# A graph-network layer on one core: three loads and one sum change their engine or their place

## The chip, the core and the metric

The kernel runs on one core of a Trainium2 chip. A time is the device time of one execution in microseconds (us). The kernel before took 1768.54 us, the median of three runs (1767.38 to 1768.69).

The engines are named as in the profile: PE is TensorE (matmuls; PEld its weight loads), DVE is VectorE, ACT is ScalarE, POOL is GpSimd, SP is SyncE. SP computes nothing here: it issues DMAs. ACT and POOL issue some as well, between their other instructions.

## The reference, cut to what matters

The input is 32 graphs of 512 nodes with 256 features, and a 0/1 adjacency matrix for each. All is float32.

```python
h = max(layernorm(x), 0)
# convolution branch: 1x1, then 17 taps along the nodes
c = relu(bn1(conv1(h)));  c = bn2(conv2(c));  x_conv = relu(c + h)
# message branch
s = h @ w_se.T + b_se                       # 3 features
A = exp(-|s_n - s_m|^2) * adj
x_nmp = A @ relu(h @ w_msg.T + b_msg)
# GRU over both
gi = concat(x_conv, x_nmp) @ w_ih.T + b_ih
gh = h @ w_hh.T + b_hh
r = sigmoid(gi_r + gh_r);  z = sigmoid(gi_z + gh_z)
n = tanh(gi_n + r * gh_n)
out = x + (1 - z) * n + z * h
```

## The kernel before, in words

The 32 graphs are worked on in two groups of 16 (`GB = 16`), and the 17-tap convolution is done in the frequency domain. The order of the instructions on each engine is the order of the Python program: inside `tc.manual_schedule()` nothing is moved. So each engine, and each DMA queue, is a list that is worked through from the front, and an instruction that waits holds back what stands behind it.

The stages, in order of time:

- **First part of group 0** (`first_part(0, ...)`, from the start to about 158 us). For each graph `b`: x is loaded (`load_x`), layer-normalised (`statistics` on DVE with one power on POOL, L370; `normalise` on DVE, L383), transposed on PE (`transpose_h`, L391), cut at zero into `hT` on DVE (L395), multiplied by conv1's weights (`conv1`, L411; the bias is added on DVE, L414) and transformed by windows (`windows_to_freq`, L426). The graphs are staggered: the statistics of graph `b + 2` are computed while graph `b` is in `conv1`. Between these, conv2's weights are transformed: 32 steps of `weights_to_freq` (eight matmuls each, L335), which the function `between(b)` deals out over the graphs. Their input comes in eight pieces (`load_taps`, L322 and L323), in two buffers of the tag `w2p`. Conv1's weights (`w1_in`, loaded by `load_w1`, L188) pass through one of these buffers too, before `scale_w1` (L269) folds the batch norm into `w1`.
- **Nodes of group 0** (about 158 to 434 us): the message branch, with the frequency-domain products of the units 0 to 35 between its steps.
- **First part of group 1** (about 432 to 550 us), with the same functions. The last four units of group 0, `u0` to `u3`, are left over, and their products (`product`, L475) are the list `left`, dealt out by `fill()`: they keep PE busy while the pipeline of group 1 fills. A product needs its weights `wt` (`load_unit`, L437, issued by SP), the sum of their two halves (`sum_unit`, POOL, L442) and the sum of two factors (POOL, L455). In the same stage the GRU's weights are loaded and combined for a fast matrix product (`combine_weights`, a list of 15 entries, called from L1225). Its entry 0 is only the load of `w_hh` (four DMAs on SP, L188); the entries behind it are sums on POOL, copies on ACT and stores.
- **Nodes of group 1** (about 550 to 831 us).
- **Gates** (from about 831 us to the end): for each of 16 pairs of graphs, 26 products (`gates_rz26`, L868), whose operands are blocks of the inputs or sums of blocks. `block_sum` computes these sums on POOL (L771 and L773). For the first pair they are ordered by `FIRST_ORDER`: nine of the part `hn`, then `inverse(0)` (L833 on PE, L837 on DVE, L839 on ACT), then the rest, which begins with `('t4', 'c')`. That is the index that the local name `ahead` holds.

SP's list around the left-over products follows from `first_part`, with `g = 1`: the load of the next x; `fill()` (the load of `u2`); another x; the store of `hT` (L396); `fill()` (the product of `u0`); `fill()` (the product of `u1` and the load of `u3`). The products store their results through ACT's queue.

## Time and profile before

| | us |
|---|---|
| median of three runs | 1768.54 |
| the profiled execution, its own time | 1767.84 |
| span of its trace, first to last instruction | 1766.1 |
| PE busy | 1749.3 (99%) |
| PE not busy | 16.8 |
| DVE, POOL, ACT busy | 1334.8, 1114.9, 674.9 |

The durations below come from the profiled execution; 1.7 us of its time lie outside the span. PE's granted clock was 0.999. Where PE is not busy can be read from a table of stages:

| stage, us | length | PE busy | DVE busy | POOL busy |
|---|---|---|---|---|
| 0 to 15 | 15 | 10.35 | 8.62 | 5.62 |
| 15 to 30 | 15 | 13.11 | 11.84 | 3.60 |
| 30 to 150 | 120 | 120.00 | 97.14 | 44.24 |
| 440 to 455 | 15 | 15.00 | 12.30 | 8.48 |
| 455 to 475 | 20 | 19.02 | 16.20 | 9.98 |
| 475 to 550 | 75 | 75.00 | 61.37 | 44.37 |
| 820 to 850 | 30 | 29.68 | 9.65 | 18.96 |
| 850 to 1700 | 850 | 850.00 | 636.62 | 532.12 |

### The profile page before, as it was taken

How to read it: one execution, taken by the hardware profiler on the slowest of the kernel's cores; microseconds unless marked ns; L12 is line 12 of the kernel's file. 1: busy time of each engine (PE TensorE's matmuls, PEld its weight loads, DVE VectorE, ACT ScalarE, POOL GpSimd, SP SyncE). 2: the span in 40 equal slices, each digit the busy share in tenths (PEclk: the TensorE clock that was granted, in tenths of full speed). 3: DMA queues.
4: the chain of work that ended last, by engine and by line, in shares of the span. 5: the costliest groups of instructions: out<-in, count | busy, mean ns of one | idle time of the engine just before them, and what ended most of it. 6: DMA issues, size and time to landing. Idle time of an engine off the chain costs nothing.

```text
span 1766.1 us, 24528 instructions
## 1 busy us (share of the span) xinstructions
PE 1749.3 (99%) x8054; PEld 1354.0 (77%) x8054; DVE 1334.8 (76%) x2621; ACT 674.9 (38%) x1543; POOL 1114.9 (63%) x1090
## 2 busy tenths in 40 slices
PE   8999999999999999999999999999999999999998
PEld 6777888888898888886877787778877787778754
DVE  7885877887896778776487778777877788777867
ACT  4556554543446445444323232223223232323221
POOL 3441787888555787777767556755766556755551
PEclk9999999999999999999999999999999999999999
DMA  9999997985779888888523453335423552345333
GB/s 250 317 297 224 246 245 225 240 224 183 260 249 221 249 237 241 225 236 278 171 71 64 116 126 93 79 80 125 121 64 67 125 126 73 70 108 125 103 59 71
DMA packets 311314, 295.16 MB, mean 167 GB/s; under 512 B 146940, under 2 KB 240668, under 8 KB 310804
## 3 DMA queue, kind: packets, MB, share of 16 engines
q1 hardware_dynamic: 301012, 265.77, 57.1%
q0 software_dynamic: 6736, 25.86, 4.6%
q10 hardware_dynamic: 3440, 1.97, 0.4%
q8 instruction: 64, 1.05, 0.3%
q14 instruction: 62, 0.51, 0.1%
HBM read 194.39 MB, written 99.16 MB: 166 GB/s over the span
## 4 chain that ended last, share of the span: by engine, by line
PE 95%; DVE 1%; POOL 1%; DMA 1%; ACT 1%; issue 0%; SPq 0%; ACTq 0%; POOLq 0%; DVEq 0%
PE pg L868 28%; PE pn L885 16%; PE py L475 12%; PE pn L630 10%; PE pm L526 6%; PE pc L411 5%; PE pc L833 5%; PE px L426 4%; PE pd L568 2%; PE pw L335 2%; PE phT L391 1%; PE pg L885 1%; PE pz L885 1%; PE psr L550 1%; DMA w<-in_w_hhT_dram 0%; POOL te L773 0%
## 5 line engine op out<-in xcount | busy, mean ns | idle before, releaser
L442 POOL TENSOR_TENSOR wsum<-wt 128x512 f32<-128x512 f32 x78 | 111.0, 1423 | 101.1 <-DMA wt<-wd 57.6
L475 PE MATMUL py<-wt,xf 128*128 128x256 f32 x640 | 154.2, 384 | 0.0
L868 PE MATMUL pg<-te,sw 128*128 128x256 f32 x600 | 154.0, 379 | 0.0
L475 PEld LDWEIGHTS py<-wt,xf 128*128 128x128 f32 x640 | 117.1, 190 | 34.9 <-issue 19.0
L859 ACT ACTIVATE rz<-rz,brz 128x256 f32<-128x256 f32 x180 | 86.3, 504 | 147.5 <-DVE rz L874 147.5
L578 DVE TENSOR_TENSOR A<-A,at 128x512 f32<-128x512 f32 x124 | 134.0, 1119 | 1.6 <-ACT A L574 1.6
L868 PEld LDWEIGHTS pg<-te,sw 128*128 128x128 f32 x600 | 114.0, 190 | 15.5
L868 PE MATMUL pg<-tn,sw 128*128 128x256 f32 x480 | 123.2, 379 | 0.0
L868 PE MATMUL pg<-hn,sw 128*128 128x256 f32 x480 | 123.2, 379 | 0.0
L885 PE MATMUL pn<-tn,sw_n 128*128 128x512 f32 x256 | 120.3, 592 | 0.0
L411 PE MATMUL pc<-w,hT 128*128 128x256 f32 x512 | 117.5, 382 | 0.9 <-DVE hT L395 0.5
L526 PE MATMUL pm<-wmsg,hq 128*128 128x259 f32 x512 | 117.5, 381 | 0.0
L1030 ACT ACTIVATE pn<-nt,vech 128x512 f32<-128x512 f32 x45 | 31.1, 692 | 218.7 <-DVE nt L1027 139.4
L411 PEld LDWEIGHTS pc<-w,hT 128*128 128x128 f32 x512 | 94.7, 190 | 23.6 <-issue 7.2
L771 POOL TENSOR_TENSOR tn<-hn 128x512 f32<-128x512 f32 x64 | 87.1, 1381 | 35.6 <-PE pn L885 35.6
L526 PEld LDWEIGHTS pm<-wmsg,hq 128*128 128x128 f32 x512 | 96.5, 189 | 14.7
L868 PEld LDWEIGHTS pg<-hn,sw 128*128 128x128 f32 x480 | 91.1, 190 | 18.3 <-PE pn L885 3.3
L370 POOL TENSOR_TENSOR rstd<-rstd,minus_half 128x4 f32<-128x4 f32 x32 | 33.3, 1041 | 108.4 <-DVE rstd L369 103.0
L868 PEld LDWEIGHTS pg<-tn,sw 128*128 128x128 f32 x480 | 91.2, 190 | 12.4
L874 DVE TENSOR_TENSOR ct<-pg,ct 128x256 f32<-128x256 f32 x180 | 74.7, 415 | 32.9 <-PE pg L868 23.5
L885 PEld LDWEIGHTS pn<-tn,sw_n 128*128 128x128 f32 x256 | 48.6, 190 | 61.2 <-issue 50.9
L833 PEld LDWEIGHTS pc<-back,yt 128*128 128x128 f32 x640 | 92.7, 190 | 1.3 <-issue 0.5
(225 smaller groups left out, 4431.4 us busy)
## 6 DMA issues: line engine op xcount, KB each, us to landing
wt<-wd SPq DMA_DIRECT2D x80, 512.0 KB, 6.8
adj<-in_adj_dram SPq DMA_DIRECT2D x128, 256.0 KB, 6.9
wd<-wst SPq DMA_DIRECT2D x64, 320.0 KB, 5.6
yd<-y SPq DMA_DIRECT2D x76, 256.0 KB, 5.8
yt<-yd SPq DMA_DIRECT2D x30, 640.0 KB, 6.2
hd<-hT SPq DMA_DIRECT2D x32, 512.0 KB, 5.2
nd<-nmp SPq DMA_DIRECT2D x32, 512.0 KB, 3.0
xb<-in_x_dram SPq DMA_DIRECT2D x128, 128.0 KB, 5.8
```

The lines of the kernel that those rows point to most:

```text
L411: nc.tensor.matmul(p[:, j, :], HT[b][:, ic, c * P : (c + 1) * P], w1[:, ic, :], start=(ic == 0), stop=(ic == DC - 1))
L442: nc.gpsimd.tensor_tensor(t, WT[g, u][:, 0], WT[g, u][:, 1], op=ALU.add)
L475: nc.tensor.matmul(dst, v[:, ic, :], w[:, ic, :], start=(ic == 0), stop=(ic == DC - 1))
L526: nc.tensor.matmul(p[:, : D + NS], hq[:, ic, c * P : (c + 1) * P], wmsg[:, ic, :], start=(ic == 0), stop=(ic == DC - 1))
L578: nc.vector.tensor_mul(A[b][:, mc, :], EXP.pop((b, mc)), AT.pop((b, mc)))
L630: nc.tensor.matmul(bk, left[:, k, :], right[:, k, :], start=(first and k == 0), stop=(k == 1), skip_group_check=True)
L771: nc.gpsimd.tensor_tensor(dst[:, k], x[:, k], y[:, k], op=op)
L833: nc.tensor.matmul(bk[:, t0:t1], YT[p][:, j, c, oc * P : (oc + 1) * P], back[:, n : n + t1 - t0], start=(c == 0), stop=(c == len(spans) - ...
L859: nc.scalar.activation(at(dst), at(src), AF.Sigmoid, bias=brz[:, o : o + 1], scale=sign)
L868: nc.tensor.matmul(bk, SW["hk"][:, k, s, :], c if k == 2 else hn[:, k], start=(onto is None and k == 0), stop=(k == K3 - 1), skip_group_ch ...
L874: nc.vector.tensor_tensor(at(dst), at(x), at(y), op=op)
L885: nc.tensor.matmul(bk[:, t], weight(q, k, o), terms[k][q][:, t], start=(first and i == 0), stop=(i == len(ks) - 1), skip_group_check=True)
```

## The change

It has four edits.

1. `load_w1` issues its four DMAs on POOL's queue instead of SP's. On POOL they stand ahead of `batch_norm("bn1")`; on SP the load of x of graph 1 and the first `load_taps` move up by four places.
2. `between` of group 0 gives graph 0 two steps of `weights_to_freq` instead of three, and graph 11 three instead of two. Of graph 0's two, one now comes ahead of the transposes of graph 1 (it was two). All steps between move one place back in the sequence.
3. Entry 0 of `combine`, the load of `w_hh`, is taken out of the list and put at the front of `left[1]`, ahead of the product of `u0`. `between` of group 1 counts from graph 2, so that the other entries stay with their graphs.
4. In `block_sum`, the one sum `('t4', 'c')` of pair 0 goes to DVE.

```diff
     def load_w1():
         t = W2P["w1"] = pools["gen"].tile([P, PI, D], FP, tag="w2p", name="w1_in", bufs=2)
-        load_rows(t[:, :DC], w1T, nc.sync)
+        load_rows(t[:, :DC], w1T, nc.gpsimd)
...
-        nc.gpsimd.tensor_tensor(dst, x, y, op=op)
+        (nc.vector if (p, name, part) == (0, *FIRST_ORDER[ahead]) else nc.gpsimd).tensor_tensor(dst, x, y, op=op)
...
-                n = (3, 0, *(3 if b == 6 else 2 for b in range(2, GB)))[b]
+                n = (2, 0, *(3 if b in (6, 11) else 2 for b in range(2, GB)))[b]
                 mine = [[steps.pop(0)] for _ in range(n)]
                 if b % 2 == 0 and b // 2 + 1 < QI // PI:
                     mine[b > 0].insert(0, partial(load_taps, gen, b // 2 + 1))
-                return (mine[0] + mine[1], mine[2:]) if b == 0 else mine
+                return (mine[0], mine[1:]) if b == 0 else mine
...
-                    return combine[b - 1] if 0 < b <= len(combine) else [], two
+                    return combine[b - 2] if 1 < b <= len(combine) + 1 else [], two
...
                 left = [[partial(load_unit, 0, u2, pools["sums"]), partial(prepare, pw, 0, u1, xf)],
-                        [partial(product, pw, 0, u0, xf), partial(prepare, pw, 0, u2, xf)],
+                        [*combine.pop(0), partial(product, pw, 0, u0, xf), partial(prepare, pw, 0, u2, xf)],
                         [partial(product, pw, 0, u1, xf), partial(load_unit, 0, u3)],
```

## The prediction

> **What bounds the kernel now.** The page first: PE is busy for 1749.3 of 1766.1 us, so everything but PE's idle 16.8 us is PE's own work, and the change removes no matmul. Then PE's waits, to find those 16.8 us.

> ```profile
> PE 1749.3 (99%) x8054; PEld 1354.0 (77%) x8054; DVE 1334.8 (76%) x2621; ACT 674.9 (38%) x1543; POOL 1114.9 (63%) x1090
> ```

> ```profile
> PE row L1133 <- DVE fr L302: 1.9, 1, 1.9
> PE phT L391 <- DVE xn L383: 1.9, 3, 1.1
> PE phT L391 <- ACT wst L345: 1.2, 1, 1.2
> PE pw L335 <- DMA w2p<-in_w2T_dram: 1.2, 1, 1.2
> ...
> PE pg L868 <- POOL tnc L773: 0.3, 1, 0.3
> ```

> The columns are total, count and longest wait. About 12 of the 16.8 us lie before the first products or behind the last ones. What the change can reach is three places. The timeline of PE in the first 32 us shows one:

> ```profile
> 9.99 3.72 PE L411 MATMUL pc<-w,hT 128*128 128x256 f32 x16 [0.50 <-DVE hT L395]
> 14.87 2.56 PE L335 MATMUL pw<-w2p,taps 17*80 17x512 f32 x16 [1.16 <-DMA w2p<-in_w2T_dram]
> ...
> 19.01 3.80 PE L411 MATMUL pc<-w,hT 128*128 128x256 f32 x16 [0.39 <-ACT wst L345]
> ...
> 29.79 1.64 PE L391 MATMUL phT<-ident,xn 128*128 128x128 f32 x8 [1.17 <-ACT wst L345]
> ```

> Behind the first conv1 PE idles 1.16 + 0.39 + 0.29 + 1.17 = 3.0 us, and never again before 165 us. The timelines of 428 to 482 us and 843 to 870 us show the others:

> ```profile
> 436.65 0.37 SPq L437 DMA_DIRECT2D wt<-wd  x1
> ...
> 445.82 1.27 POOL L442 TENSOR_TENSOR wsum<-wt 128x512 f32<-128x512 f32 x1 [0.39 <-DMA wt<-wd]
> ...
> 446.61 1.89 PE L475 MATMUL py<-wt,xf 128*128 128x256 f32 x8
> ...
> 464.17 1.28 POOL L1225 TENSOR_TENSOR w<-w 128x128 f32<-128x128 f32 x3 [4.69 <-DMA w<-in_w_hhT_dram]
> ...
> 469.45 0.69 PE L391 MATMUL phT<-ident,xn 128*128 128x128 f32 x2 [0.59 <-DVE xn L383]
> ...
> 847.82 0.70 PE L868 MATMUL pg<-tnc,sw 128*128 128x256 f32 x2 [0.32 <-POOL tnc L773]
> ```

> POOL waits 4.69 us for `w_hh`; the power L370 stands behind its sums, DVE's normalise behind that, and PE loses 0.98 us (20 less the 19.02 busy from 455 to 475). At 847.8 PE loses 0.32 us to the sum t4/c. Note also the last left-over weights: issued at 436.65, landed only at 445.7, used at 446.61. That load has 0.9 us to spare.

> [...] conv1's four issues hold SP from 1.67 to 4.90. [...] POOL's taps issued at 13.63 moved no packet until 17.0, when SP's backlog had run out; later the two queues shared. [...] The trace has the DVE product L578 at about 0.65 us (two in 1.29) and, beside POOL, at 1.75.

> **The start: conv1's weights and the moved step.** Removed from SP: 3.2 us of issue. The x of graph 1 leaves at 1.67 instead of 4.94, the first taps at 2.2 to 4.8 instead of 5.4 to 8.1. Added on POOL: four issues at 0.58 (row L322, 2.33 us for four), from about 1.3 to 3.6. Queued behind them is `batch_norm("bn1")`, which began at 3.26 on its vectors' arrival: it slips by some 0.4 us (0.6 if the first issue takes 0.74, as at 13.63). ACT takes its result at 4.85, so the row sums come some 0.4 later than 6.67; `scale_w1` uses them at 8.59. Covered. The x of graph 1 now competes with the second half of graph 0's x on ACT's queue at 3 to 4 us; I charge 0.3 us (0 to 0.6) to the chain from x to conv1.

> If conv1's weights land in time, by hand: conv1(0) runs 10.3 to 14.0. Graph 1's x is there, so its statistics follow hT at 10.25 (before: 0.76 us later, at 10.70, for the DMA), the power ends at 13.25, normalise 13.3 to 14.7. On PE: one step (1.03 us, from 1.10 for eight) 14.0 to 15.05, without the wait of 1.16, as the taps land about 3 us earlier, also if conv1's weights take 1 us of their bandwidth; the transposes of graph 1 to 16.1. DVE adds conv1(0)'s bias (1.28) to 15.95 and makes hT(1) to 17.3: PE idles 1.25 us and starts conv1(1) at 17.35. The second step ends at 22.0. On DVE the statistics of graph 2 run 17.3 to 19.2, POOL's power to 20.3, normalise to 21.75; bias to 23.0, statistics of graph 3 to 24.9, hT(2) to 26.2, normalise(3) to 27.6. PE's transposes of graph 3 therefore end near 28.4 and conv1(2) begins at 28.3, against 31.26. PE has then done one step less, 1.03 us, which it does at graph 11, where it is 100% busy. Gain: 31.26 - 28.3 - 1.03 = **1.9 us**. Behind that DVE still leads PE: xn(4) stood ready 2.6 us ahead of its use at 38.12, and PE moves up on DVE by some 0.9.

> The moved steps make the taps of pieces 2 and 3 wait for the last step on the old buffer, now behind conv1(2) and conv1(4). Queued behind them on POOL are a load of x and the power. Their issue slips from 34.1 to about 36 and from 49.6 to 53.9; the second delays the power at 57.18 by 1.0 us, its normalise at 58.86 by 0.5. DVE idles 0.96 + 0.42 us per graph there, and PE takes that xn only at about 65. Cost nothing; if that cover failed, under 1 us.

> Will conv1's weights land in time? `scale_w1` is due at 8.9. The landing times of the first 30 us:

> ```profile
> w2p<-in_w2T_dram SPq DMA_DIRECT2D x4, 128.0 KB, 7.0
> w2p<-in_w2T_dram POOLq DMA_DIRECT2D x4, 128.0 KB, 8.5
> ...
> w_in<-in_w1T_dram SPq DMA_DIRECT2D x4, 64.0 KB, 2.9
> ```

> The last POOL issue is at about 3.0. POOL's first packet came 1.6 us after issue on a quiet queue (444.61), 3.6 and 4.9 us after it behind a full SP queue (13.63, 812.79). With 0.7 us for the data and 0.8 to 2.6 to completion that gives 6.1 to 11.2. Lateness is paid in full, since hT, conv1 and graph 1's statistics stand behind `scale_w1` on DVE. Bounds: 0 to 2.3 us; I take 0.4, as the load leaves before the queues are full. **Start: -1.5 us**, from -2.2 to +0.7.

> **The load of w_hh.** It goes onto SP between the hT store (435.97) and the last left-over load (436.65). Four issues take 2.28 us, but the bytes matter more. From 433.0 to 443.4 the DMA engines moved 3.43 MB at 330 GB/s without a break, in SP's order, and the last left-over load was last. 786 KB ahead of it take 2.0 us at the best rate there, about 400 GB/s, or 3.7 us at the 211 GB/s of 459 to 462 us, where `w_hh` itself was moving. The load then lands at 447.7 to 449.4. PE waits for it from 446.61: 1.1 to 2.8 us, and 0.3 more for POOL's two sums (1.27 + 0.73), which now begin at the landing. Middle: 2.3 us lost. Queued behind on POOL are a load of x and the power of graph 19, which have the same delay as PE. Given back: POOL's 4.69 and PE's 0.98 us. **Sum: +1.3 us**, from +0.4 to +2.1; if the transfers don't delay that load at all, -1.0.

> **The first gate sum.** POOL takes 1.27 us for it, 846.50 to 847.77. [...] DVE's two-input 128x512 operations take 0.65 to 0.75. On DVE it starts at 843.55, behind the last L837 and the relu that it reads, and ends by 844.3, by 845.3 [...]. DVE's next operation is at 849.96. **-0.3 us**, with ends of -0.32 and 0; POOL's other sums come 1.3 us earlier and stay ahead of PE.

> **Sum:** -1.5 + 1.3 - 0.3 = -0.5 us: 1767.84 becomes 1767.3. The profiled execution is 0.7 below the median of 1768.54, so in medians **1768.0 us**. A measurement of this kernel can tell about 0.2% from no change, 3.5 us: this is no change.

> **Rivals.** *Late weights, slower.* POOL's load waits behind x and the taps, as at 13.63, and the last left-over load pays the full 3.7 us. For: both POOL loads behind a full queue moved nothing for 3 us. Against: only x is queued when this one leaves. At the bounds: +0.7 + 2.1 - 0.3 = +2.5, 1771.0. Each us of landing after 8.9 costs one: -1.9 + 0.1 + 2.1 - 0.3 = 0 puts the turn at 9.0, and +3.5 at 12.5. *No new wait, faster.* The DMA engines overlap w_hh's narrow transfers with their neighbours' and conv1's weights are early: -2.2 - 1.0 - 0.3 = -3.5, 1765.0. For: DMA busy shares of 0.8 to 0.9 in that stage, so not quite full. Against: the load had only 0.9 us to spare. *DVE as the bound at the start*: the early loads change nothing, because DVE works without a gap from 22.5 to 43; then the start gives 0, and the sum is +1.0, 1769.5. Against: its gapless stretch begins with hT(1), which waits on PE.

> **Numbers.** No change as worked out, with DVE's rival inside it: 0.67. Late weights: 0.2, all counted as slower, since a landing after 12.5 or a cost that I don't see would carry it over 3.5 us. No new wait: 0.13, all counted as faster, since it ends on the bound. The ends of the likeliest case's own terms, taken two thirds together, span 1766.5 to 1770.0. The range for all cases reaches from the faster one to 1 us beyond the late one: 1764.8 to 1772.0.

> **What would show it.** Right: pw at about 14 without a wait on w2p; conv1(2) near 28.3; a new PE wait of 1 to 3 us on `wt` near 447; no wait at 469; none on tnc. Wrong: `scale_w1` waiting for w_in; the product at 446.6 on time; conv1(2) near 30.2 (nothing won).

## The result, and the profile after

The kernel after takes **1771.34 us** (median of 13; 1769.43 to 1776.41), the kernel before in the same comparison 1768.38 (13 runs). The ratio is 1.0019 with an interval of [1.0012, 1.0026]: **slower, by about 3.3 us**, or 0.19%. A second comparison gave 1771.89 against 1768.98, ratio 1.0017 [1.0008, 1.0025]. The forecast was 1768.0, no change.

The profiled execution of after is its fastest (1769.43 us, span 1767.7, clock 0.998), so its trace can account for 1.6 us of the loss (1767.7 less the 1766.1 of before's span) and not for all of it. Its page shows the same bound as before, with the same matmuls:

```profile
PE 1749.6 (99%) x8054; PEld 1354.9 (77%) x8054; DVE 1340.4 (76%) x2622; ACT 674.1 (38%) x1543; POOL 1114.6 (63%) x1093
```

PE's waits (total, count, longest) show what is new:

```profile
PE pc L411 <- DVE hT L395: 2.9, 2, 2.6
PE row L1133 <- POOL ident masks.py:199: 2.5, 1, 2.5
PE py L475 <- DMA wt<-wd: 2.5, 1, 2.5
PE phT L391 <- DVE xn L383: 0.9, 1, 0.9
```

The third line is the wait that was forecast. The first is not: conv1(0) waits 2.6 us for hT, where it waited 0.5. The second is PE's start: POOL now makes `ident` behind its first DMA issue, at 2.19 instead of 1.02. It costs nothing by itself, as the run with SP held (below) has it too and begins conv1(0) at 9.73. The waits on w2p and on tnc are gone. The timeline of the first 36 us says what hT stood behind. A line of a timeline gives start and length in us, the engine (SPq is SP's issue of a DMA), the line of the kernel, the operation, output<-inputs with shapes, and in brackets how long the engine was idle before and what ended that:

```profile
1.38 0.70 POOL L188 DMA_DIRECT2D w_in<-in_w1T_dram  x1 [0.41 <-issue]
1.66 0.43 SPq L192 DMA_DIRECT2D x<-in_x_dram  x1
2.44 1.63 POOL L188 DMA_DIRECT2D w_in<-in_w1T_dram  x3
3.18 1.87 SPq L322 DMA_DIRECT2D w2p<-in_w2T_dram  x4
...
11.43 0.75 DVE L269 TENSOR_TENSOR w<-w_in,row 128x256 f32<-128x256 f32 x2 [2.02 <-DMA w_in<-in_w1T_dram]
...
12.84 5.41 PE L411 MATMUL pc<-w,hT 128*128 128x256 f32 x16 [2.60 <-DVE hT L395]
...
18.18 1.10 PE L335 MATMUL pw<-w2p,taps 17*80 17x512 f32 x8
...
31.80 3.62 PE L411 MATMUL pc<-w,hT 128*128 128x256 f32 x16
```

`scale_w1` waits 2.02 us for conv1's weights and runs at 11.43, not at 8.6. conv1(0) begins at 12.84 (before: 9.99), and it takes 5.41 us where the same sixteen matmuls took 3.72. The table of stages gives the reason. Behind the stretch and its length it has the busy time of PE, PEld, DVE, ACT and POOL, then PE's granted clock, the busy share of the DMA engines and their GB/s:

```profile
12.00:14.00 2.00, 1.16 (x3) 0.98 (x4) 2.00 (x6) 0.00 (x0) 0.00 (x0) 0.73 0.99 258
14.00:16.00 2.00, 2.00 (x7) 1.55 (x6) 0.84 (x7) 0.00 (x0) 1.34 (x2) 0.50 0.99 309
16.00:18.00 2.00, 2.00 (x10) 1.62 (x8) 1.68 (x5) 0.28 (x1) 2.00 (x5) 0.92 0.96 271
```

Behind the wait PE runs at half its clock, in the clock's records from 12.91 to 16.33: 3.41 us, in which 1.7 us of matmul time is lost. So conv1(2) begins at 31.80 (before 31.26; forecast 28.3), although a step less of `weights_to_freq` stands ahead of it. Group 0's first part ends 2.19 us later than before.

The second place, on the timeline of 430 to 482 us:

```profile
438.21 5.57 SPq L188 DMA_DIRECT2D w<-in_w_hhT_dram  x4
...
444.84 0.38 SPq L437 DMA_DIRECT2D wt<-wd  x1
...
450.82 1.97 PE L475 MATMUL py<-wt,xf 128*128 128x256 f32 x8 [2.48 <-DMA wt<-wd]
450.85 1.26 POOL L442 TENSOR_TENSOR wsum<-wt 128x512 f32<-128x512 f32 x1 [3.60 <-DMA wt<-wd]
...
463.08 1.37 POOL L1225 TENSOR_TENSOR w<-w 128x128 f32<-128x128 f32 x3
```

The last left-over load leaves at 444.84 instead of 436.65, since the four issues ahead of it hold SP for 5.57 us. PE waits 2.48 us for it. From group 1's first transposes (435.21; before 433.63, so 1.58 late on arrival) to those at 453.82 (before 449.20) the lag grows by 3.04 us. POOL's sums at 463.08 wait for nothing, where they had waited 4.69 us, and PE has no wait at 469: 1.9 us come back. Group 1's first part ends at 552.82, 2.69 us late. The third place, the first pair of gates:

```profile
846.14 1.10 DVE L773 TENSOR_TENSOR tnc<-cp 128x512 f32<-128x512 f32 x1
846.66 1.71 POOL L773 TENSOR_TENSOR te<-hn,te 128x512 f32<-128x512 f32 x1
```

The sum starts when the forecast said, 843.5 by before's time, and POOL's neighbour takes 1.71 instead of 1.27; the sum itself takes 1.10, within the forecast's 0.75 to 1.75 (the upper end is the time of the product L578 beside POOL). PE waits for neither; the lag shrinks from 2.67 to 2.04.

### The profile page after: what moved, and what is told of

Its sections match the earlier page's. It is cut to its first block, busy times and chain, and to the rows that moved or that the text cites. A ratio compares the mean times of both kernels' runs of the same rounds, so it can differ in the third digit from the quotient of the medians.

```text
span 1767.7 us, 24523 instructions
## 1 busy us (share of the span) xinstructions
PE 1749.6 (99%) x8054; PEld 1354.9 (77%) x8054; DVE 1340.4 (76%) x2622; ACT 674.1 (38%) x1543; POOL 1114.6 (63%) x1093
## 3 DMA queue, kind: packets, MB, share of 16 engines
q8 instruction: 64, 1.05, 0.2%
## 4 chain that ended last, share of the span: by engine, by line
PE 96%; DVE 1%; DMA 1%; issue 0%; POOL 0%; ACT 0%; SPq 0%; POOLq 0%; ACTq 0%; DVEq 0%
PE pg L868 29%; PE pn L885 16%; PE py L475 11%; PE pn L630 10%; PE pm L526 6%; PE pc L411 6%; PE pc L833 5%; PE px L426 4%; PE pd L568 2%; PE pw L335 2%; PE phT L391 1%; PE pg L885 1%; PE pz L885 1%; PE pn L613 1%; PE psr L550 1%; DMA w_in<-in_w1T_dram 0%
## 5 line engine op out<-in xcount | busy, mean ns | idle before, releaser
L442 POOL TENSOR_TENSOR wsum<-wt 128x512 f32<-128x512 f32 x78 | 111.3, 1427 | 102.8 <-DMA wt<-wd 62.3
L475 PE MATMUL py<-wt,xf 128*128 128x256 f32 x640 | 154.2, 384 | 2.5 <-DMA wt<-wd 2.5
L868 PE MATMUL pg<-te,sw 128*128 128x256 f32 x600 | 154.0, 379 | 0.0
L475 PEld LDWEIGHTS py<-wt,xf 128*128 128x128 f32 x640 | 117.1, 190 | 37.6 <-issue 19.0
L578 DVE TENSOR_TENSOR A<-A,at 128x512 f32<-128x512 f32 x124 | 134.2, 1120 | 1.2 <-ACT A L574 1.0
L868 PEld LDWEIGHTS pg<-te,sw 128*128 128x128 f32 x600 | 114.0, 190 | 15.5
L868 PE MATMUL pg<-tn,sw 128*128 128x256 f32 x480 | 123.2, 379 | 0.0
L868 PE MATMUL pg<-hn,sw 128*128 128x256 f32 x480 | 123.2, 379 | 0.0
L411 PE MATMUL pc<-w,hT 128*128 128x256 f32 x512 | 119.2, 386 | 2.9 <-DVE hT L395 2.9
L411 PEld LDWEIGHTS pc<-w,hT 128*128 128x128 f32 x512 | 95.9, 192 | 26.2 <-issue 5.6
L526 PEld LDWEIGHTS pm<-wmsg,hq 128*128 128x128 f32 x512 | 96.5, 189 | 14.7
L868 PEld LDWEIGHTS pg<-hn,sw 128*128 128x128 f32 x480 | 91.1, 190 | 18.3 <-issue 3.3
L868 PEld LDWEIGHTS pg<-tn,sw 128*128 128x128 f32 x480 | 91.2, 190 | 12.4
L370 POOL TENSOR_TENSOR rstd<-rstd,minus_half 128x4 f32<-128x4 f32 x32 | 33.3, 1042 | 105.1 <-DVE rstd L369 104.7
## 6 DMA issues: line engine op xcount, KB each, us to landing
xb<-in_x_dram SPq DMA_DIRECT2D x128, 128.0 KB, 6.0
```

Source lines behind the costliest of these rows:

```text
L411: nc.tensor.matmul(p[:, j, :], HT[b][:, ic, c * P : (c + 1) * P], w1[:, ic, :], start=(ic == 0), stop=(ic == DC - 1))
L442: nc.gpsimd.tensor_tensor(t, WT[g, u][:, 0], WT[g, u][:, 1], op=ALU.add)
L475: nc.tensor.matmul(dst, v[:, ic, :], w[:, ic, :], start=(ic == 0), stop=(ic == DC - 1))
L526: nc.tensor.matmul(p[:, : D + NS], hq[:, ic, c * P : (c + 1) * P], wmsg[:, ic, :], start=(ic == 0), stop=(ic == DC - 1))
L578: nc.vector.tensor_mul(A[b][:, mc, :], EXP.pop((b, mc)), AT.pop((b, mc)))
L868: nc.tensor.matmul(bk, SW["hk"][:, k, s, :], c if k == 2 else hn[:, k], start=(onto is None and k == 0), stop=(k == K3 - 1), skip_group_ch ...
```

## The experiments

Each kernel was compared with the kernel before on the same chip. The differences are of means, since they are added up below; the error is one standard error. Clock is the mean over all executions. It also counts half clock behind the last matmul (in before's profile PE ends at 1757.6 and the clock falls at 1762.7), where PE has no work. So it is a mark and not a count of half-clock windows: both at 0.998, after's first profile has one between (12.9 to 16.3) and that of edit 2 alone has none.

| kernel | median, us | ratio to before | difference of means, us | clock (before) |
|---|---|---|---|---|
| edit 1 alone | 1770.72 | 1.0008 [1.0001, 1.0014] | +1.3 ± 0.4 | 0.9971 (0.9974) |
| edit 3 alone | 1771.29 | 1.0009 [1.0001, 1.0017] | +1.5 ± 0.5 | 0.9970 (0.9974) |
| edit 4 alone | 1767.83 | 0.9990 [0.9982, 0.9999] | -1.6 ± 0.4 | 0.9976 (0.9974) |
| edit 2 alone | 1767.12 | 0.9990 [0.9983, 0.9997] | -1.8 ± 0.5 | 0.9983 (0.9974) |
| after without edit 1 | 1767.89 | 0.9989 [0.9982, 0.9995] | -1.7 ± 0.4 | 0.9983 (0.9971) |
| after, w_hh behind the last load | 1768.21 | 0.9990 [0.9982, 0.9998] | -1.5 ± 0.4 | 0.9977 (0.9971) |
| both of these | 1765.28 | 0.9976 [0.9969, 0.9983] | -4.1 ± 0.5 | 0.9982 (0.9971) |
| after, PE kept busy ahead of conv1(0) | 1770.50 | 1.0009 [1.0000, 1.0018] | +0.9 ± 0.6 | 0.9977 (0.9971) |
| conv1's weights on ACT, w_hh behind | 1766.14 | 0.9986 [0.9979, 0.9992] | -2.7 ± 0.4 | 0.9981 (0.9975) |
| "both", PE kept busy at the start | 1766.35 | 0.9985 [0.9979, 0.9992] | -2.7 ± 0.4 | 0.9985 (0.9975) |
| before, PE kept busy at the start | 1768.42 | 1.0000 [0.9992, 1.0008] | -0.4 ± 0.4 | 0.9984 (0.9975) |
| after, once more | 1771.89 | 1.0017 [1.0008, 1.0025] | +2.9 ± 0.6 | 0.9968 (0.9975) |
| after, SP's list held | 1767.99 | 0.9992 [0.9984, 1.0000] | -1.5 ± 0.5 | 0.9984 (0.9971) |

### The four edits one by one

Edit 1 alone, the kernel before with

```diff
-        load_rows(t[:, :DC], w1T, nc.sync)
+        load_rows(t[:, :DC], w1T, nc.gpsimd)
```

> The kernel before with the first edit alone: conv1's weights on POOL's queue. Theory: the load lands near 11.4 us as in the changed kernel, scale_w1 on DVE waits 2 us for it, conv1 of graph 0 starts near 12.8 instead of 9.99, and PE, idle for 2.6 us, runs part of that conv1 at half clock (5.4 instead of 3.7 us). Less the 1.16 us wait on the taps, which is hidden behind it, the first part of group 0 ends 2.5 to 3.5 us later and the time is +3 us (2 to 4.5). Rival: the load alone is harmless, and the changed kernel's late start comes from the two steps in another order: then within 1 us of the kernel before.

Measured: +1.3 us, below the 2 to 4.5 of the theory and just above the rival's 1. In its profile the weights land so that `scale_w1` runs at 11.75, behind a wait of 2.6 us, and conv1(0) begins at 13.15, 3.16 late, at half clock. The wait of 1.16 us for the taps behind it is gone, as they have landed meanwhile. So with the old order of steps a part of the lateness falls into waits that were there before. The same holds for the clock: its mean falls by 0.0003 only, as the kernel before has half-clock windows of its own in many executions (last section). This profile has two of them (from 13.9 and from 34.4), and its first part ends 4.12 us late (162.12 against 158.00), more than the mean.

Edit 3 alone:

```diff
-                    return combine[b - 1] if 0 < b <= len(combine) else [], two
+                    return combine[b - 2] if 1 < b <= len(combine) + 1 else [], two
...
-                        [partial(product, pw, 0, u0, xf), partial(prepare, pw, 0, u2, xf)],
+                        [*combine.pop(0), partial(product, pw, 0, u0, xf), partial(prepare, pw, 0, u2, xf)],
```

> The kernel before with the load of w_hh moved ahead alone. Theory: the last left-over load is issued some 6 us later and PE waits 2.5 us for it near 449, products and transposes behind it are 3.0 us later; the stall near 469 goes and gives back 1.8 us; sum +1.2 us (0.5 to 2). Rival: the wait at 449 only appears because the changed kernel's start shifted the DMAs; then no wait and -1.8 us.

Measured: +1.5 us, near the forecast's +1.3. Its timeline shows the wait, and the price of the wait beyond its length:

```profile
450.34 3.22 PE L475 MATMUL py<-wt,xf 128*128 128x256 f32 x8 [2.45 <-DMA wt<-wd]
```

These eight matmuls take 3.22 us instead of 1.89: here too the clock is halved, from 450.9 to 454.3. In after's own profile it stays full at this place, in those of after without edit 1 and of after with PE kept busy it does not (448.0 and 448.4).

Edit 4 alone:

```diff
-        nc.gpsimd.tensor_tensor(dst, x, y, op=op)
+        (nc.vector if (p, name, part) == (0, *FIRST_ORDER[ahead]) else nc.gpsimd).tensor_tensor(dst, x, y, op=op)
```

> The kernel before with the sum t4/c of pair 0 on DVE alone. Theory: the 0.32 us wait of PE on tnc goes, -0.3 to -0.5 us, about what a measurement can just tell; the trace shows PE without a wait there. Rival: [...] POOL's next sums are as late as before and the wait moves to another sum: 0.

Measured: -1.6 ± 0.4 us. Its trace shows only 0.63 of that between the first gates and `inverse` of the second pair, the same as in after. Both expectations were smaller. What the other microsecond is stays open; nothing in the trace explains it.

Edit 2 alone:

```diff
-                n = (3, 0, *(3 if b == 6 else 2 for b in range(2, GB)))[b]
+                n = (2, 0, *(3 if b in (6, 11) else 2 for b in range(2, GB)))[b]
...
-                return (mine[0] + mine[1], mine[2:]) if b == 0 else mine
+                return (mine[0], mine[1:]) if b == 0 else mine
```

> The kernel before with the moved step alone (two steps at graph 0, three at graph 11), conv1's weights still on SP. By the working of the prediction without its early loads: the wait of 1.16 us on the taps stays, but hT of graph 1 and all behind it come 1 to 2 us sooner, and the pipeline catches up the step; the first part of group 0 ends 0.5 to 1.5 us earlier, time -0.8 us. Rival: DVE sets the pace from 22 to 43 us whatever PE does first, and the moved step is just paid later: 0 to +1 us.

Measured: -1.8 us, more than the 0.8 that was expected. conv1(2) begins at 27.82 in its profile, 3.44 earlier than before, which less one step of 1.03 is 2.4 us won, with conv1's weights and the taps on SP as they were. It does not last: between conv1(2) and conv1(3) 1.05 us of it go, as PE's transposes and its second step there run late, the transposes behind a wait on the copy `wst`:

```profile
35.10 1.14 PE L391 MATMUL phT<-ident,xn 128*128 128x128 f32 x8 [0.26 <-ACT wst L345]
36.17 1.63 PE L335 MATMUL pw<-w2p,taps 17*80 17x512 f32 x8
37.73 3.72 PE L411 MATMUL pc<-w,hT 128*128 128x256 f32 x16
```

In the kernel before this conv1(3) begins at 40.12. The first part ends at 156.64 against 158.00, 1.36 us earlier, within the 0.5 to 1.5 that was expected. The moved step needs none of edit 1. And the clock rises: 19 of its 21 executions have a mean of 0.998 or more, against 24 of 57 of the kernel before.

The four sum to -0.6 us, and the whole change gives +2.9. So they do not simply add up. Edits 2, 3 and 4 sum to -1.9; the next kernel has just these.

### After without edit 1; after with w_hh behind the last load; both

Without edit 1 is one line back to `nc.sync`. For the second, entry 0 of `combine` goes behind the load of `u3`:

```diff
-                        [*combine.pop(0), partial(product, pw, 0, u0, xf), partial(prepare, pw, 0, u2, xf)],
-                        [partial(product, pw, 0, u1, xf), partial(load_unit, 0, u3)],
+                        [partial(product, pw, 0, u0, xf), partial(prepare, pw, 0, u2, xf)],
+                        [partial(product, pw, 0, u1, xf), partial(load_unit, 0, u3), *combine.pop(0)],
```

> The changed kernel with conv1's weights back on SP's queue, nothing else. Theory: their late landing is what costs at the start. scale_w1 waits for nothing, conv1 of graph 0 starts near 10, PE stays at full clock over the first 30 us, and the first part of group 0 ends 1.4 us before that of the kernel before, as with the moved step alone; with the load of w_hh still ahead (+1.5) and the sum on DVE (-0.6) the time is -1 us against before (-2 to +0.5), 4 us under the changed kernel. Rival: the late start comes from the order of the steps, and the time stays within 1 us of the changed kernel.

> The changed kernel with the load of w_hh behind the load of the last left-over unit on SP's queue instead of ahead of it (end of the third entry of the list of left-over work). Theory: the order of these two loads is the whole loss there. PE has no wait on wt near 449 and none on xn near 469, the first part of group 1 is 1.5 to 2 us shorter than before, and the time is 2.5 us under the changed kernel, +1 us against before (0 to 2). Rival: the DMA engines are the limit in that stage, so that w_hh delays some other load just as much: within 0.7 us of the changed kernel.

> The moved step and the sum on DVE as in the change, conv1's weights on SP as before, and the load of w_hh behind the last left-over load. If the three theories hold, this has all three gains and neither loss: -1.8 (step), -1.0 (stall at 469; up to -1.8) and -0.6 (sum): -3.4 us against before (-2.5 to -4.5). Rival: the gains cover each other (a later start had hidden part of the stalls): -1.5 us.

Without edit 1 the difference is -1.7: the other three add up, and edit 1 in their company costs 2.9 + 1.7 = 4.6 us, not 1.3. The clock suggests that the moved step is what it meets badly: that step alone raises the mean clock to 0.9983, and where edit 1 joins it the clock is 0.9968. This is not shown, since no run has these two edits alone. With w_hh behind the last load the loss of 2.9 turns into -1.5, a gain of 4.4 us where 2.5 was expected, though in its profile conv1(0) is as late as in after (12.85). Both together give **1765.28 us, the fastest of all, and faster than either kernel**, within what was expected. Its timeline around the left-over products:

```profile
436.97 0.40 SPq L437 DMA_DIRECT2D wt<-wd  x1
...
437.42 6.59 SPq L188 DMA_DIRECT2D w<-in_w_hhT_dram  x4
...
446.88 1.89 PE L475 MATMUL py<-wt,xf 128*128 128x256 f32 x8
```

The last load leaves ahead of w_hh, the product waits for nothing, and POOL's sums find w_hh there at 460.51 all the same. Edit 3 carried a gain; its place on SP's list cost more than the gain.

### PE kept busy ahead of conv1(0)

The kernel after with three matmuls that nothing reads:

```diff
+    WARM = 3
...
             if b == b0:
+                if g == 0:
+                    idle = bank("idle")
+                    for _ in range(WARM):
+                        nc.tensor.matmul(idle[:, : 2 * P], ident, fr.rearrange("p c g k -> p (c g k)")[:, : 2 * P], start=True, stop=True)
                 conv1(b)
```

> The changed kernel with three idle matmuls (some 2.3 us, into a bank of their own) on PE between the transposes and conv1 of graph 0, where PE waits for conv1's weights. Theory: PE's clock halves because it idles there; with the idle matmuls conv1 of graph 0 takes 3.7 instead of 5.4 us, no half-clock window shows before 20 us, and the time is 1 to 2 us under the changed kernel, +1.8 against before. Rival: the half clock is no matter of that wait, or its loss is hidden behind DVE: within 0.7 us of the changed kernel.

Measured: +0.9 us, 2.0 ± 0.9 under the kernel after, and the clock goes from 0.9968 to 0.9977. In its profile the clock is full from its first record at 8.1 us to 448.4, and conv1(0) takes 3.62 us. But in that execution conv1's weights had also landed by 10.14, so that the profile alone does not part the two. The mean over all executions speaks for the clock: 0.0009 of 1768 us is 1.6 us.

### Conv1's weights on ACT's queue

After with w_hh behind the last load, and

```diff
-        load_rows(t[:, :DC], w1T, nc.gpsimd)
+        load_rows(t[:, :DC], w1T, nc.scalar)
```

> The kernel after with conv1's weights issued on ACT's queue instead of POOL's, and the load of w_hh behind the last left-over load. It tells POOL's queue itself from the mere fact that the four issues stand on another queue than SP's. Theory (POOL's own path of transfers is what is late): on ACT the weights land like the loads on SP, 3 to 4 us after issue; ACT issues them behind its two halves of x, so at 3 to 5.5 us, and they land at 7 to 9.5, against 11.4 on POOL. conv1(0) then begins at 9.7 to 10.8 and the time is within 1 us of the kernel with these weights on SP: 1764.5 to 1766.5. Rival (the DMA engines are full with x and the taps, whoever issues): landing at about 11, conv1(0) near 12.8, PE's clock halved behind the wait, 1768 to 1769.

The time fits the first theory (1766.14 us, and a full clock at the start), the landing does not: `scale_w1` runs at 9.92 and conv1(0) begins at 11.33, between what the two expectations said. The answer of the trace on the tile w_in, in this kernel (time from issue to landing of the four loads):

```profile
DMA to landing us min/median/max: 5.7/5.9/6.1
```

In the kernel after:

```profile
L188 POOL DMA_DIRECT2D w_in<-in_w1T_dram x4: 541/559/702, 1.4 to 3.5; - x4
DMA to landing us min/median/max: 4.1/5.9/7.8
```

On SP in the kernel before it was 1.8 to 3.2. So a load on ACT's queue is as slow as one on POOL's in the middle, and POOL's own path is not what these have in common. In common is that SP, freed of four issues, sends the x of graph 1 (512 KB) and the taps (4 x 128 KB) earlier than in the kernel before: at 1.67 and from 2.90, not at 4.94 and from 5.41 (in after at 1.66 and from 3.18).

### Matmuls without a reader in the waits of "both" and of before

Two of them behind conv1(0) in both kernels (`idle_a`), then one ahead of conv1(1) in "both", and two ahead of the transposes of graph 3 in the kernel before:

```diff
                 conv1(b)
+                if g == 0:
+                    idle = bank("idle_a")
+                    for _ in range(2):
+                        nc.tensor.matmul(idle[:, : 2 * P], ident, fr.rearrange("p c g k -> p (c g k)")[:, : 2 * P], start=True, stop=True)
                 one, two = between(0) if g == 0 else ([], [])
```

> The version with conv1's weights on SP, the moved step, w_hh behind the last left-over load and the sum on DVE, and in addition three matmuls without a reader: two behind conv1(0), in PE's wait of 1.46 us for the taps, and one ahead of conv1(1), in its wait of 0.89 us. Each takes about 0.49 us. Theory (PE's short waits at the start still cost half-clock windows in some executions, 4 of 22 had a mean clock under 0.998): such executions become rarer, mean lower by 0.2 to 0.8 us than this version without them, 1764.7 to 1765.3. Rival (the clock at the start is no matter any more): the same time within 0.3 us, or 0.3 us more where a matmul is longer than the wait.

> The kernel before with four matmuls without a reader: two behind conv1(0), in the wait of 1.16 us for the taps, and two ahead of the transposes of graph 3, in the wait of 1.17 us. No load and no order changes. It tests whether the spread of the kernel before comes from PE's clock at the start. Theory (the waits between 14 and 31 us let the clock fall to a half for one or two windows of 3.41 us, 1.7 us of matmul time each, in most executions: 33 of 57 had a mean clock under 0.998): under a quarter of the executions stay under 0.998, and the mean falls by 1.0 to 1.6 us, to about 1768.2; that is most of what the moved step alone won (1.8 us). Rival (the clock falls for a reason outside these waits): the share under 0.998 stays above 0.5, and the mean is the same within 0.4 us or 0.3 more.

In "both" they bring nothing: clock 0.9985 against 0.9982, and the gain over before is 2.7 instead of 4.1 us. Neither expectation held, and why it is less stays open. In the kernel before the clock answers as the theory said: 1 of 13 executions is under 0.998, against 31 of 62. The time answers less than it said: -0.4 ± 0.4 us. In its profile the matmuls are a little longer than the waits (conv1(1) at 19.28 for 19.01), which is 0.3 us. The clock's 0.0008 would be worth 1.5 us; about 0.8 ± 0.5 of it is not found. Reckoned by executions, the gain comes out: those of the kernel before under 0.998 take 1.9 us more than the others, and (31/62 - 1/13) x 1.9 is 0.8 us, less 0.3 is 0.5. That the waits at the start bring the clock down is shown; what it costs is less sure than the product of clock and time makes it.

### The kernel after, once more

> The kernel after once more, beside the others, for the size of the loss and for its scatter. If its parts add up as measured one by one (conv1's weights on POOL, which beside the moved step cost 1771.34 - 1767.89 = 3.5 us; the rest -1.75), it is 1.7 us over the kernel before at the least; its own first comparison gave 3.3 with an interval of 2.1 to 4.6. I expect 2 to 3.5 us over the kernel before, and that the mean clock of its executions lies between 0.995 and 0.998.

Measured: +2.9 ± 0.6 us, mean clock 0.9968, both as expected. Its profiled execution has two half-clock windows, 6.83 us from 11.07 on, and in it x of graph 0 is late as well: the statistics of its last part begin at 8.57, behind a wait for x of 3.8 us, where the kernel before has them at 5.3 and after's first profile at 6.0. `scale_w1` waits only 0.45 us for conv1's weights here, as DVE comes to it late. So what is late at the start, x or the weights, changes between executions.

### POOL's path, or what SP sends meanwhile

The kernel after, with four loads of 64 bytes a row in the place on SP that conv1's weights had:

```diff
             load_w1()
+            hold = consts.tile([P, DC, 16], FP, name="hold")
+            load_rows(hold, w1T[:, :16], nc.sync)
             load_x(1)
```

> The kernel after, and in addition four loads on SP of 64 bytes a row (16 KB in all, to a tile that nothing reads), at the place where the kernel before had conv1's weights. They hold SP's list for about 3.2 us, so that the x of graph 1 and the first taps leave at 4.9 and 5.4 as before, not at 1.7 and 3.2, while conv1's weights stay on POOL. Theory (the weights are late because the x of graph 1 and the taps, which leave earlier now, fill the DMA engines ahead of them: on ACT's queue they took 5.9 us as well): the weights land by 7.5 to 8.5, the sum that scales them does not wait or waits under 0.5 us, conv1(0) begins at 10 to 10.8, and the time falls by 2 to 3.5 us against the kernel after, to 1768 to 1769.5. Rival (POOL's own path is slow, whatever else is on the way): the weights land at 11 or later, conv1(0) begins near 12.8, and the time is that of the kernel after or up to 1 us more, since the taps are late too: 1771 to 1773.

The first theory held, and with more than it asked. The trace on w_in and the timeline of the start:

```profile
DMA to landing us min/median/max: 3.1/3.3/3.4
```

```profile
1.66 2.79 SPq L188 DMA_DIRECT2D hold<-in_w1T_dram  x4
2.43 1.65 POOL L188 DMA_DIRECT2D w_in<-in_w1T_dram  x3
...
4.50 0.43 SPq L192 DMA_DIRECT2D x<-in_x_dram  x1
4.97 2.33 SPq L322 DMA_DIRECT2D w2p<-in_w2T_dram  x4
...
8.33 0.74 DVE L269 TENSOR_TENSOR w<-w_in,row 128x256 f32<-128x256 f32 x2
...
9.73 3.72 PE L411 MATMUL pc<-w,hT 128*128 128x256 f32 x16 [0.50 <-DVE hT L395]
```

POOL issues at the same instants as in after, the weights land in 3.3 us, `scale_w1` waits for nothing, and conv1(0) begins at 9.73 at full clock. The packets of POOL's queue run from 3.4 to 6.0 us here, and from 3.5 to 9.4 in after. The x of graph 0 is in time as well (its last statistics end at 5.27). With -1.5 ± 0.5 us the kernel is where after without edit 1 is (-1.7). So POOL's queue cost nothing by itself that these runs can tell. **It was the 3.2 us that SP gained: SP used them to issue 1 MB sooner, and the 256 KB that were due first landed in 5.9 us instead of 3.3 (medians of the four loads).** A later half-clock window, from 17.6 us on, is in this profile too: conv1(1) takes 5.41 us, and the first part ends at 157.91, only 0.09 before that of the kernel before.

The lateness has two parts. The packets of POOL's queue are spread over 5.9 us in after and over 2.6 with SP held. And from the last of them to the landing (the last issue at 3.5 plus its 7.8 or 3.4) it is 1.9 us in after and 0.9 with SP held. No run separates what causes the one from what causes the other.

## Why the prediction was wrong

**What bounds the kernel** was read rightly: PE alone, in three places, and all that moved was in these three.

**The start: forecast -1.5, and here it failed**, in the term for the landing of conv1's weights; in after's profile the first part ends 2.19 us late instead. The estimate ran from 6.1 to 11.2 us and 0.4 us of lateness was taken, "as the load leaves before the queues are full", and "only x is queued when this one leaves". But the working had itself moved the x of graph 1 to 1.67 and the first taps to 2.2 to 4.8, between and right behind POOL's issues. The early taps were entered as a gain, and the competition was charged 0.3 us to the chain of x and nothing to the weights. They landed at 11.3, 2.4 us behind the due time of 8.9, just beyond the end of the bounds that the text gave its lateness (0 to 2.3). The charge on x was too small as well: x was 0.7 late in after's first profile and 3.3 in the second. The run with SP held takes both away and does not part them. The sign of being wrong that the forecast named, `scale_w1` waiting for w_in, is in both profiles (2.02 and 0.45 us).

**A term was missing: PE's clock.** Before's profile showed a full clock over the start, and no price was set on a wait beyond its length. In after's two profiles waits of 2.6 and 2.7 us are followed by half clock. The clock's records hold 0.5 and 1.0 alone; ahead of the end of the matmuls the stretch at 0.5 lasts 3.41 us in the first of these profiles and 6.83 in the second. What follows a wait goes with where it lies in steps of that length. Count steps of 3.413 us, the length of after's record, back and forth from a change of the clock in a profile. A step with 2.3 to 2.7 us of idle PE was followed by a half-clock step in all seven cases: at the start in after's two profiles, in edit 1 alone and with w_hh behind, and at the left-over product in edit 3 alone, without edit 1 and with PE kept busy. In after's two profiles and with SP held the same wait at the product fell across two steps, at most 1.5 us in each, and the clock stayed full. Here are the steps of edit 3 alone, then those of after, in the columns of the table of stages:

```profile
447.48:450.89 3.41, 0.96 (x7) 0.70 (x6) 2.91 (x8) 0.47 (x2) 0.52 (x1) 1.00 1.03 350
450.89:454.31 3.42, 3.42 (x10) 2.70 (x9) 0.36 (x2) 0.66 (x2) 2.16 (x3) 0.50 0.69 252
...
446.40:449.82 3.42, 1.94 (x13) 1.52 (x12) 2.18 (x7) 1.71 (x4) 0.85 (x2) 1.00 1.01 330
449.82:453.23 3.41, 2.35 (x10) 1.79 (x11) 1.93 (x5) 0.41 (x2) 2.38 (x3) 1.00 0.64 247
```

So 2.3 us of idle PE in a step of 3.41 was enough. Idle time in the step does not explain all of it: half clock also came behind steps with 0.1 to 1.2 us of idle PE (near 17 us in edits 3 and 4 alone and with SP held, at 34 us in edit 1 alone); what marks these stays open. What the clock cost can be told roughly: against after without edit 1 the mean clock is down by 0.0014, 2.5 us of 1768, and the run with PE kept busy won 2.0 ± 0.9 back. That is about half of the 4.6 us that edit 1 costs there. The rest is left for the wait itself.

**The moved step** was right in sign, and larger at conv1(2) than forecast: 1.9 us were forecast, its own profile has 2.4 (27.82, forecast 28.3). But the forecast let PE lose nothing behind conv1(2), and 1.05 us went there, so that 1.36 reached the end of the first part. That the early taps were needed for it was wrong: with the taps on SP as before it gains as well (-1.8 alone, -1.7 beside edits 3 and 4, where PE still waits 0.93 us for them). Its slipping taps for pieces 2 and 3 cost nothing that a run showed.

**The load of w_hh: forecast +1.3, measured +1.5 ± 0.5** alone, and in after's trace 3.04 lost and 1.9 given back. The agreement is in part luck: the forecast had 2.3 lost and 1.0 given back, and the errors of the two cancel. The wait of 2.48 lies in the forecast 1.1 to 2.8; by before's time the load landed at about 449.2, in the forecast 447.7 to 449.4. The issues took 5.57 us, not 2.28, so the load left at 444.84, 8.19 us later than before. From there to the start of its product it is 6.0 us, where before it took 9.0 to land. How much of the 6.0 went to waiting behind the bytes of w_hh is not shown. The half clock behind the wait, in some executions, was not foreseen.

**The first gate sum: forecast -0.3**, trace -0.63, runs -1.6 ± 0.4. Sign and place were right, the size was too small, and not all of it is explained: the runs' further microsecond may not be the sum's.

**Of the rivals**, *Late weights, slower* is what happened, at 1771.0 for a measured 1771.3; its mechanism, a load held up by x and the taps, is what the run with SP held shows (3.3 us to landing with these sent later, 5.9 in after). The landing of 12.5 from which it was to be over 3.5 us was set without the clock: with it 11.3 is near enough. That its sum fits is luck: it had +0.7, +2.1 and -0.3 for the three places, and after's trace has +2.19, of which 0.6 is won back by 435 us, +1.1 and -0.63. *No new wait* and *DVE as the bound* did not occur. The forecast also took 0.2% as the least that a measurement can tell; the intervals here are 0.07% to either side, so that 0.19% is a change and not none.

## What to carry to other kernels

## What was not expected of the hardware

The kernel before owes part of its scatter to PE's clock: in three comparisons 33 of 57, 37 of 59 and 31 of 62 executions have a mean under 0.998, and these take 1770.1 to 1770.7 us on average, the others 1768.0 to 1768.2. The profile that the forecast was made from has a full clock. And the same kind of issue can hold SP for very different times: the four for w_hh took 2.28 us in the kernel before, 5.57 in after and 6.59 in "both", the four for conv1's weights in the kernel before 3.23.
